# A two-layer kernel on one core: two places for the softmax's scores, half banks for the second layer's products on half chunks, and the causal mask by a select on GpSimd

## The chip, the cores and the metric

One core of one Trainium2 chip runs the whole program. The metric is device time in microseconds, from launch to the end on that core. The engines are TensorE (PE, with its weight loads as PEld), VectorE (DVE), ScalarE (ACT), GpSimd (POOL) and the queues that issue DMAs (SP's above all, and POOL's).

## The reference

The input is 2048 positions of width 128, all float32. Two layers follow each other, each with a mixer and a feed-forward part, a layernorm before each and a residual around each:

```
x = x + ssd(layernorm(x))            # layer 0: gated state-space mixer, 8 heads of 32, state 16
x = x + attention_and_experts(layernorm(x))
    # causal attention, 16 heads of 8, over all 2048 positions;
    # then 8 experts 128 -> 512 -> 128 with gelu, all computed, weighted by the two best gates
x = x + mamba(layernorm(x))          # layer 1: selective scan, inner width 128*2, state 16
x = x + ternary_ffn(layernorm(x))    # silu(x w1) * (x w2), then h1, gelu, h2, gelu, w3
```

In the attention, scores = q.k / sqrt(8), the entries with key after query are masked, softmax is taken over the keys, and the weighted sum of v follows.

## The kernel before, in words

The positions are cut into four chunks of C = 512 columns (NC = 4), each of four blocks of 128. All values stay on the chip. Every stage is written as a Python function that records operations in a `Program`: `ssd(c)`, `prepare(c)` (layernorm, q, k and v), `shift(c, g)` (the largest score of each query for head group g), `weighted(c, g)` (scores again, exp, sum over keys), `conclude(c)` (output projection), `experts(c)`, `scan(c, part)` (the selective scan on half a chunk, H = 256 columns) and `feed(c)`. The class `Order` then plays the program: it ranks every operation by the longest chain behind it, takes at each step the operation that can start first on its engine, and writes out one static order for each engine. `issue` at line 638 emits them, which is why nearly all rows of the profile carry L638. Each engine then runs its list in order, held only by semaphores.

Tiles get their memory from places. A `Tag` has a number of places, and an operation that allots a tile waits in the plan until one is free. SBUF places belong to pools: "first" (ssd), "second" (experts, scan), "attention" and "last" (feed, and a few extra tiles of scan). "second" opens when the last ssd operation is done, "last" when the last attention operation is done.

PSUM has eight banks of 512 float32 columns. The function `seat` deals them out: tag m (maxima, projections) has one place of two banks, e (scores that go to exp) one place of two banks, o (sums over keys) one bank, and a, b and c one bank each. Tag a may use banks a and b, and the banks of m while no m tile is asked for; tag c may use bank c, and those of e and o in the same way.

In `shift`, for each block of 128 queries and each chunk of keys, two thin products (32 rows deep, one for each of two heads) go into an m tile, and DVE takes the maximum over the keys. In `weighted`, for each block of 128 keys and each pair of heads, an e tile gets the thin score products, the shift by a second pair of products with `sh`, and on the diagonal a bfloat16 product with `mask_kq` that adds -1e30 where the key is after the query; ACT makes `probs` of it by exp, and four products of 128 rows by 9 columns add to o (`sum_up`). There are 320 such e tiles, 128 of them on a diagonal, 32 in each chunk.

`experts(c)` runs 8 experts in pairs on 512 columns: 4 products, 4 gelus, 4 products that accumulate, for each expert. The gelus of a pair form a batch, within which ACT takes no exp. `feed(c)` has 8 products from w1 and w2, then 16 from h1, 16 from h2, and 16 of 128 columns from w3. `scan(c, part)` runs 16 state steps: exp on ACT (`sda`), a product and two scans on DVE (`sdb`), a copy of the last state on POOL, and a DMA from POOL that adds the step's result to one of two sums (`sL`).

Of the kernel before, what the change touches and what calls it, by code (L numbers as in the profile page):

```python
# [76 lines left out]
class Place:  # L77


    def __init__(self, pool, banks=None, lent=None, real=None):  # L80
        self.pool, self.lent, self.real = pool, lent, real
        self.user, self.free = None, 0.0
        self.banks = banks or (self,)


class Tile_:


    def __init__(self, tag, shape, dtype, name, real=None):
        self.tag, self.shape, self.dtype, self.name, self.real = tag, tuple(shape), dtype, name, real  # L90
        self.log, self.first, self.place, self.left, self.last = [], None, None, 0, 0.0
        self.pe = None
        self.ops = set()
# [104 lines left out]
class Op:  # L198
    __slots__ = (
        "n", "engine", "calls", "deps", "time", "after", "table", "batch", "allots", "tiles",  # L200
        "rank", "waits", "outs", "start", "end", "ready",
# [3 lines left out]
class Program:  # L205
# [5 lines left out]
    def __init__(self, nc):  # L211
        self.nc, self.ops, self.tags, self.joined, self.batching = nc, [], {}, None, None
        for e in self.ENGINES:
            setattr(self, e, Engine(self, e))
# [14 lines left out]
    def add(self, engine, method, args, kw):  # L229
# [12 lines left out]
        for v, w in [(v, False) for v in reads] + [(v, True) for v in writes]:  # L242
# [21 lines left out]
            t.ops.add(op)  # L264
            op.tiles.add(t)
# [6 lines left out]
    def new(self, engine, table=None):  # L272
# [4 lines left out]
        op.n, op.deps, op.allots, op.tiles = len(self.ops), {}, [], set()  # L277
        self.ops.append(op)
        return op
# [104 lines left out]

class Order:
# [8 lines left out]
    def settle(self):  # L394
# [36 lines left out]
        for op in ops:  # L431
            for t in op.allots:
# [22 lines left out]
    def rank(self):  # L455
        ops = self.p.ops
        outs = {o: [] for o in ops}
        for o in ops:
# [3 lines left out]
            o.ready = 0.0  # L462
# [30 lines left out]
        for o in reversed(order):  # L493
# [5 lines left out]
            o.rank = r + o.after  # L499

    def possible(self, op):

        at, seen, taken = 0.0, {}, set()
        for t in op.allots:
# [7 lines left out]
            for pl in tag.places:  # L512
                if pl in taken or any(b.user is not None or b in taken for b in pl.banks):
                    continue
# [19 lines left out]
    def play(self):  # L534
        free = {e: 0.0 for e in Program.ENGINES}
        cand = {e: [] for e in Program.ENGINES}
# [13 lines left out]
        while len(self.order) < n:  # L550
            best = None
            for e, ops in cand.items():
# [3 lines left out]
                for o in ops:  # L556
                    at = max(free[e], o.ready)
# [10 lines left out]
                    if at < least:  # L568
                        least = at
                    pick.append((at, o))  # L570
                if not pick:
                    continue
                o = max((o for at, o in pick if at <= least + 1e-6), key=lambda o: self.key(o, open_batch))
# [8 lines left out]
            at, o = best  # L582
            e = o.engine
            cand[e].remove(o)
            for t in o.allots:
                t.tag.wanted -= 1
            if o.allots:
                self.possible(o)
                for t in o.allots:
                    t.tag.given += 1  # L590
                    for b in t.place.banks:
                        b.user = t
# [11 lines left out]
            o.start = at  # L604
            free[e] = at + time
            o.end = at + time - o.time + o.after
# [12 lines left out]
            for d, full in o.outs:  # L619
                d.waits -= 1  # L620
                d.ready = max(d.ready, o.end if full else o.start)
                if d.waits == 0:
                    enter(d)
            self.order.append(o)
        self.span = max(o.end for o in self.order)

# [14 lines left out]
SWITCH, BOOST = 1.28, 40.0  # L641
# [3 lines left out]
def two_layers(ctx: ExitStack, tc: tile.TileContext, a: dict, out: bass.AP):  # L645
# [19 lines left out]
    def banks(tag, bank, lent=None, width=1, shared=False):  # L665
        t = nc.tag(tag, width * C, True, shared)
        t.places.append(Place(None, bank.banks if isinstance(bank, Place) else tuple(bank), lent, None))
        return t.places[-1]

    pairs_ = {k: ps.tile([P, 2 * C], F32, name=f"ps_{k}") for k in ("m", "e")}  # L670
    single = {k: ps.tile([P, C], F32, name=f"ps_{k}") for k in ("o", "a", "b", "c")}
    bank = {}
    for k, t in pairs_.items():
        for j in range(2):
            bank[f"{k}{j}"] = Place(None, real=t[:, j * C : (j + 1) * C])
    for k, t in single.items():
        bank[k] = Place(None, real=t)

    def seat(tag, names, lent=None, width=1, shared=False, whole=None):
        t = nc.tag(tag, width * C, True, shared)  # L680
        pl = Place(None, tuple(bank[n] for n in names), nc.tags[lent] if lent else None)
        pl.real = whole if whole is not None else bank[names[0]].real
        t.places.append(pl)

    seat("m", ("m0", "m1"), width=2, whole=pairs_["m"])
    seat("e", ("e0", "e1"), width=2, whole=pairs_["e"])
    seat("o", ("o",))
    for n in ("a", "b"):
        seat("a", (n,), shared=True)
    for n in ("m0", "m1"):  # L690
        seat("a", (n,), "m", shared=True)
    seat("c", ("c",), shared=True)
    for n in ("e0", "e1"):
        seat("c", (n,), "e", shared=True)
    seat("c", ("o",), "o", shared=True)
# [51 lines left out]
    select(mask_kq, [[1, P]], 0, -1, ALU.is_ge, MASKED)  # L747
    before8 = const("before8", (P, NE, NE))
# [8 lines left out]
    LN = [("st", NB * 6, 2), ("mv", NB * 2, 2), ("rs", NB, 2)]  # L757
# [8 lines left out]
    def layernorm(z, dst, src, width=D):  # L766
# [3 lines left out]
        rs = tile_(f"rs_{z}", (P, nb))  # L770
        for b in range(nb):
# [3 lines left out]
        nc.gpsimd.tensor_tensor(rs, rs, minus_half[:, 0:nb], ALU.pow)  # L775
        for b in range(nb):
            nc.vector.tensor_scalar(
                dst[:, b, :], src[:, b, :], mv[:, b, 0:1], rs[:, b : b + 1], ALU.subtract, ALU.mult
            )
# [19 lines left out]
    for tag, words, n in (  # L799
        ("nx", NB * D, 1), ("nTa", C, 1), ("hi", C, 2), ("os", C, 2), ("sh", C, 2), ("qR", 2 * C, 3),  # L800
# [34 lines left out]
    def prepare(c):  # L835
        xn = xa[c] = tile_("xa", (P, NB, D))
# [6 lines left out]
        nc.vector.tensor_scalar(nT, pt, col("ln1_w"), col("ln1_b"), ALU.mult, ALU.add)  # L843
        qR = []
        for g in range(0, NG, 2):
            qR.append(tile_("qR", (P, 2, C), F32R))
            for w, n, dst in ((w_k, "k", kR[c][g // 2]), (w_q, "q", qR[-1])):
                pf = tile_("m" if n == "k" else "e", (P, 2, C))
                for j in range(2):
                    nc.tensor.matmul(pf[:, j], w[:, g + j], nT, start=True, stop=True)  # L850
                    hi = tile_("hi", (P, C), F32R)
                    nc.scalar.activation(hi, pf[:, j], AF.Identity, bias=col(f"b{n}", g + j))
                    nc.tensor.matmul(pf[:, j], minus[n], hi, start=False, stop=True, skip_group_check=True)
                    nc.vector.tensor_scalar(dst[:, j], pf[:, j], col(f"b{n}", g + j), None, ALU.add)
# [9 lines left out]
        held[c] = [q[:, j] for q in qR for j in range(2)]  # L864
# [4 lines left out]
    def shift(c, g):  # L869
        qR = held[c][g]  # L870
# [27 lines left out]
        nc.vector.tensor_copy(sh, pm)  # L898
        held[c, g] = sh

    def weighted(c, g):
        qR = held[c][g]
# [13 lines left out]
        for kb in range(nk):  # L916
# [3 lines left out]
            for i in range(0, 4, 2):  # L920
                pss = tile_("e", (P, 2, C))
                with nc.together(0.11 + 2 * (C - q0) / 2400.0 + 0.1 * diag):
# [4 lines left out]
                    for j in range(2):  # L927
                        hr = slice(32 * (i + j), 32 * (i + j) + 32)
                        nc.tensor.matmul(pss[:, j, q0:], onesR[hr], sh[hr, q0:], start=False, stop=not diag)
                    for j in range(2 * diag):  # L930
                        nc.tensor.matmul(pss[:, j, q0 : q0 + P], ident16, mask_kq, start=False, stop=True)
# [3 lines left out]
                )  # L935
                prs.append(pr)
# [5 lines left out]
        nc.vector.tensor_copy(os, po)  # L942
        pa = tile_("a", (P, NB, 4, HD + 1))
# [9 lines left out]
    def conclude(c):  # L953
        att = held.pop(("att", c))
        pt = transposed(att.rearrange("p b g i d -> p b (g i d)"), "a")
        aT = tile_("os", (P, C))
        nc.vector.tensor_copy(aT, pt)
# [6 lines left out]
    def attentions():  # L964
# [3 lines left out]
        for (c, g), nxt in zip(jobs, jobs[1:] + [None]):  # L968
            if g == 2 and c + 1 < NC:
# [42 lines left out]
    def ssd(c):  # L1012
# [516 lines left out]
```

## Time and profile before

| what | value |
|---|---|
| time, median of 3 runs | 1730.93 us (1716.0 to 1738.16) |
| the profiled execution, its own time | 1727.12 us |
| its span, first to last instruction | 1725.4 us |
| mean granted TensorE clock | 0.785 |
| PE busy | 1503.1 us (87%), 6350 matmuls |
| PEld busy | 670.9 us (39%) |
| DVE busy | 994.8 us (58%) |
| ACT busy | 642.9 us (37%), 56 table loads |
| POOL busy | 326.4 us (19%) |
| DMA | 91.75 MB, mean 53 GB/s |

A float32 product appears as two matmul instructions in the counts, and its operands' shapes as rows*columns of the weights and partitions x columns of what streams. Busy time of TensorE counts time in which a product is under way, at whatever clock. The granted clock is the share of full speed that the throttle gave.

### The profile page before, as it was taken

How to read it: one execution, taken by the hardware profiler on the slowest of the kernel's cores; microseconds unless marked ns; L12 is line 12 of the kernel's file. 1: busy time of each engine (PE TensorE's matmuls, PEld its weight loads, DVE VectorE, ACT ScalarE, POOL GpSimd, SP SyncE). 2: the span in 40 equal slices, each digit the busy share in tenths (PEclk: the TensorE clock that was granted, in tenths of full speed). 3: DMA queues.
4: the chain of work that ended last, by engine and by line, in shares of the span. 5: the costliest groups of instructions: out<-in, count | busy, mean ns of one | idle time of the engine just before them, and what ended most of it. 6: DMA issues, size and time to landing. Idle time of an engine off the chain costs nothing. (4 is left out here: it accounts for less than half of the span.)

```text
span 1725.4 us, 17368 instructions
## 1 busy us (share of the span) xinstructions
PE 1503.1 (87%) x6350; PEld 670.9 (39%) x6350; DVE 994.8 (58%) x1874; ACT 642.9 (37%) x873; POOL 326.4 (19%) x458
## 2 busy tenths in 40 slices
PE   6899998999999998899998899899877679995738
PEld 3554554455423343333333243233322234442323
DVE  4556557665545468667867656775454551256641
ACT  2221421432334426445453433454445433234311
POOL 4321310310000111212311111121031221103320
PEclk9887987996879959987865655799565569997769
DMA  2000000000112102524402311341042543134730
GB/s 86 1 1 1 1 1 1 1 1 1 42 36 61 51 1 56 123 67 87 97 7 46 60 36 35 95 110 42 13 84 56 99 110 98 49 114 106 157 88 6
DMA packets 77334, 91.75 MB, mean 53 GB/s; under 512 B 7040, under 2 KB 47776, under 8 KB 77248
## 3 DMA queue, kind: packets, MB, share of 16 engines
q1 hardware_dynamic: 59536, 58.11, 11.4%
q0 software_dynamic: 17280, 31.46, 10.7%
q10 hardware_dynamic: 432, 1.06, 0.2%
q8 instruction: 50, 0.82, 0.2%
q14 instruction: 36, 0.29, 0.1%
HBM read 57.90 MB, written 1.25 MB: 34 GB/s over the span
## 5 line engine op out<-in xcount | busy, mean ns | idle before, releaser
L638 DVE TENSOR_REDUCE top_a_None<-ps_m 128x2 f32<-128x1024 f32 (+3 forms) x320 | 339.7, 1062 | 285.0 <-PE ps_m L638 278.4
L638 ACT ACTIVATE probs_attention<-ps_e 128x1024 f32<-128x1024 f32 (+3 forms) x320 | 286.5, 895 | 526.9 <-PE ps_o L638 281.2
L638 PE MATMUL ps_e<-qR_attention,w_kR_attention 32*128 32x512 f32 (+3 forms) x640 | 187.8, 581 | 82.5 <-ACT probs_attention L638 80.9
L638 PE MATMUL ps_m<-w_kR_attention,qR_attention 32*128 32x512 f32 (+3 forms) x640 | 178.3, 546 | 17.4 <-DVE top_a_None L638 16.1
L638 PE MATMUL ps_o<-probs_attention,w_vv_attention 128*9 128x512 f32 (+3 forms) x1152 | 182.6, 712 | 0.2 <-ACT probs_attention L638 0.2
L638 POOL DMA_DIRECT2D sL_second<-sdb_second x114 | 99.2, 885 | 385.6 <-DVE sdb_second L638 328.6
L638 PEld LDWEIGHTS ps_e<-qR_attention,w_kR_attention 32*128 32x128 f32 x640 | 74.0, 227 | 237.9 <-ACT probs_attention L638 187.5
L638 DVE TENSOR_TENSOR_SCAN sdb_second<-sda_second,w_hlast_None,sdb_second 128x256 f32<-128x256 f32 x212 | 149.6, 739 | 7.7 <-ACT sda_second L638 5.4
L638 PEld LDWEIGHTS ps_m<-w_kR_attention,qR_attention 32*128 32x128 f32 x640 | 71.6, 217 | 211.8 <-issue 67.9
L638 PE MATMUL ps_e<-sh_attention,w_onesR_attention 32*128 32x512 f32 (+3 forms) x640 | 148.6, 459 | 0.0
L638 PE MATMUL ps_c<-h_second,fc_second 128*128 128x512 f32 x208 | 114.9, 654 | 0.6 <-DVE ye_second L638 0.6
L638 ACT ACTIVATE sda_second<-sL_second 128x512 f32<-128x512 f32 x120 | 72.7, 624 | 31.8 <-DVE sdb_second L638 18.6
L638 ACT ACT_TABLE_LOAD x56 | 71.8, 1283 | 30.2 <-PE ps_a L638 18.6
L638 DVE TENSOR_TENSOR sdb_second<-sL_second,sbb_second 128x512 f32<-128x512 f32 x101 | 68.0, 680 | 24.0 <-DMA sL_second<-sdb_second 11.1
L638 PEld LDWEIGHTS ps_e<-sh_attention,w_onesR_attention 32*128 32x128 f32 x640 | 80.8, 249 | 0.5
L638 POOL TENSOR_TENSOR acc_second<-acc_second,ye_second 128x512 f32<-128x512 f32 x28 | 36.5, 1305 | 231.3 <-DVE ye_second L638 229.8
L638 PE MATMUL ps_a<-enT_second,fc_second 128*128 128x512 f32 x128 | 77.0, 686 | 3.1 <-ACT h_second L638 2.2
L638 ACT ACTIVATE h_second<-ps_a,cols 128x512 f32<-128x512 f32 x64 | 44.0, 687 | 63.3 <-PE ps_a L638 63.2
L638 POOL COPY w_hlast_None<-sdb_second 128x2 f32<-128x2 f32 x99 | 55.6, 570 | 23.8 <-DVE sdb_second L638 23.5
L638 PE MATMUL ps_b<-enT_second,fc_second 128*128 128x512 f32 x98 | 58.8, 686 | 0.9 <-ACT h_second L638 0.8
L638 PE MATMUL ps_m<-fh_last,hw_last 128*128 128x512 f32 x120 | 58.3, 608 | 0.2 <-DVE sW_second L638 0.2
L638 PEld LDWEIGHTS <-ident 128*128 128x128 bf16 x512 | 30.6, 101 | 61.7 <-issue 50.0
(430 smaller groups left out, 2094.3 us busy)
## 6 DMA issues: line engine op xcount, KB each, us to landing
sL_second<-sdb_second POOLq DMA_DIRECT2D x114, 256.0 KB, 3.6
fc_second<-in_fc SPq DMA_DIRECT2D x64, 256.0 KB, 2.6
sbb_second<-scratch_b SPq DMA_DIRECT2D x112, 128.0 KB, 3.0
gb_second<-scratch_g SPq DMA_DIRECT2D x32, 256.0 KB, 3.3
hw_last<-in_h SPq DMA_DIRECT2D x8, 1024.0 KB, 5.3
w_last<-in_w SPq DMA_DIRECT2D x12, 256.0 KB, 3.9
sbb_last<-scratch_b SPq DMA_DIRECT2D x16, 128.0 KB, 3.4
sL_second<-sdb_last POOLq DMA_DIRECT2D x6, 256.0 KB, 4.2
```

What stands on the lines that cost most here:

```text
L638: getattr(engine, method)(*args, **kw)
```

## The change

It has these parts.

1. PSUM: m keeps two banks, e gets four (two places of two banks), o one, and one bank is lent to nobody. Tags b and c are gone. Tag a is a whole bank, a new tag d is half a bank (256 columns): each bank's two halves are places of their own, with the other as `mate`. The planner starts no product in a half while an accumulation is open in its mate. Both may borrow the banks of m, e and o.
2. The products of `experts` and `feed` run on half chunks, `experts(c, part)` and `feed(c, part)`, in d tiles; weights are loaded for each half, those of `feed` in pieces of 512 columns (tag fw, three places). `feed`'s tiles get places in pool "second" too.
3. The mask products of `weighted` go. After exp, on a diagonal, `select` on GpSimd sets the entries with key after query to 0 in the 128 columns that need it, for both heads in one instruction of 128 x 256.
4. DVE work moves: the normalising step of every layernorm becomes an ACT activation with scale and bias, for which GpSimd computes -mean * rstd in two small operations; copies and bias additions out of PSUM (nT, q and k, sh, os, aT, and scan's in_b, bd, dt_b, z) become ACT operations; scan's multiplication with D goes to GpSimd.
5. `prepare` computes only the first two head groups' q and k; `project(c, 2)` does the others when the chunk's first group is weighted, and qR has two places in place of three. scan has two sda and three sdb tiles in "second" (before: three and four), and more in "last".
6. `Order` models TensorE by a class `Array`: shapes, weight loads under products, the time lost between shapes, and a clock that halves when little was done in a window. When it holds thin or other small shapes it stays with that shape if it can. Its further switches (FILL, PAIR, ZMIN, BURST, FAST) are all off.

The core of the diff:

```diff
-    seat("m", ("m0", "m1"), width=2, whole=pairs_["m"])
-    seat("e", ("e0", "e1"), width=2, whole=pairs_["e"])
+    seat("m", ("m0", "m1"), whole=wide["m"])
+    for j in (0, 2):
+        seat("e", (f"e{j}", f"e{j + 1}"), whole=wide["e"][:, j * C : (j + 2) * C])
     seat("o", ("o",))
...
+    for n, lent in (("a", None), ("m0", "m"), ("m1", "m"), ("e3", "e"), ("e2", "e"), ("e1", "e"), ("e0", "e"), ("o", "o")):
+        seat("a", (n,), lent)
+        for half in range(2):
+            seat("d", (n,), lent, half)
...
     def possible(self, op):
...
+                if op.starts and any(b.mate is not None and b.mate.open for b in pl.banks):
+                    continue
...
     def layernorm(z, dst, src, width=D):
...
+        nc.gpsimd.tensor_tensor(nm, mv[:, :, 0], rs, ALU.mult)
+        nc.gpsimd.tensor_scalar(nm, nm, -1.0, None, ALU.mult)
         for b in range(nb):
-            nc.vector.tensor_scalar(
-                dst[:, b, :], src[:, b, :], mv[:, b, 0:1], rs[:, b : b + 1], ALU.subtract, ALU.mult
+            nc.scalar.activation(
+                dst[:, b, :], src[:, b, :], AF.Identity, bias=nm[:, b : b + 1], scale=rs[:, b : b + 1]
             )
...
     def weighted(c, g):
...
-                        nc.tensor.matmul(pss[:, j, q0:], onesR[hr], sh[hr, q0:], start=False, stop=not diag)
-                    for j in range(2 * diag):
-                        nc.tensor.matmul(pss[:, j, q0 : q0 + P], ident16, mask_kq, start=False, stop=True)
+                        nc.tensor.matmul(pss[:, j, q0:], onesR[hr], sh[hr, q0:], start=False, stop=True)
                 pr = tile_("probs", (P, 2, C))
                 nc.scalar.activation(
                     pr[:, :, q0:], pss[:, :, q0:], AF.Exp, scale=float(1.0 / np.sqrt(np.float32(HD)))
                 )
+                if diag:
+                    select(pr[:, :, q0 : q0 + P], [[0, 2], [1, P]], 0, -1, ALU.is_ge, 0.0)
...
         for (c, g), nxt in zip(jobs, jobs[1:] + [None]):
+            if g == 0:
+                project(c, 2)
...
-        ("second", "gb", C, 2), ("second", "ye", C, 2), ("second", "fc1", FF, 2), ("second", "fc2", FF, 2),
-        ("second", "h", C, 8), ("last", "h", C, 4),
+        ("second", "gb", H, 3), ("second", "ye", H, 2), ("second", "fc1", FF, 2), ("second", "fc2", FF, 2),
+        ("second", "h", H, 8), ("last", "h", H, 8), ("last", "fc1", FF, 2), ("last", "fc2", FF, 2), ("last", "gb", H, 2),
...
-        ("last", "fxn", NB * D, 1), ("last", "fnT", C, 1), ("last", "w12", 2 * FF, 1), ("last", "w3", NF * D, 1),
-        ("last", "fs", C, 2), ("last", "fh", C, 8), ("last", "hw", 4 * FF, 2), ("last", "res", NB * D, 1),
+        ("second", "fxn", H, 1), ("second", "fnT", H, 1), ("second", "fw", FF, 3), ("last", "fw", FF, 3),
+        ("second", "fs", H, 2), ("second", "fh", H, 8), ("last", "fh", H, 8), ("last", "fxn", H, 1),
...
                     for f in range(NF):
-                        ph = tile_("a", (P, C))
+                        ph = tile_("d", (P, H))
...
     for c in range(NC):
-        experts(c)
+        for part in range(SPLIT):
+            experts(c, part)
         for part in range(SPLIT):
             scan(c, part)
-        feed(c)
+            feed(c, part)
```

## The prediction, made before the changed kernel ran

> **What bounds the kernel now.** I read the page's busy table first, then its forty slices, then busy time by stage, the waits of TensorE, and last the time order in the poorest stage. The slices show TensorE at nine tenths almost everywhere up to the last quarter, with a granted clock that swings between five tenths and full:
>
> ```profile
> PE   6899998999999998899998899899877679995738
> PEclk9887987996879959987865655799565569997769
> ```
>
> I cut the span where work starts and ends in the trace: the layernorm of experts(0), the end of each chunk's attention (xa is updated at 355, 640, 1036 and 1395 us), and the tail. Columns: stretch, its length, then busy us (instructions) of PE, PEld, DVE, ACT, POOL, then granted clock, DMA share, GB/s.
>
> ```profile
> 90.00:500.00 410.00, 386.50 (x2051) 203.87 (x2052) 250.12 (x540) 126.66 (x178) 67.81 (x84) 0.83 0.03 8
> 500.00:603.00 103.00, 100.55 (x430) 36.80 (x430) 48.21 (x58) 44.95 (x53) 8.89 (x7) 0.95 0.19 52
> 603.00:862.00 259.00, 236.51 (x1012) 93.98 (x1012) 188.29 (x320) 122.09 (x164) 53.87 (x81) 0.80 0.32 71
> 862.00:1118.00 256.00, 230.46 (x942) 89.07 (x944) 171.26 (x282) 104.67 (x132) 34.80 (x59) 0.59 0.21 45
> 1118.00:1214.00 96.00, 93.58 (x406) 35.50 (x398) 59.74 (x89) 46.49 (x57) 22.53 (x29) 0.94 0.30 75
> 1214.00:1396.00 182.00, 134.78 (x546) 49.77 (x546) 88.95 (x161) 79.97 (x108) 36.34 (x58) 0.55 0.31 61
> 1396.00:1492.00 96.00, 86.64 (x208) 38.01 (x209) 29.44 (x73) 28.52 (x41) 18.53 (x19) 0.92 0.36 102
> 1492.00:1672.00 180.00, 121.99 (x365) 61.66 (x363) 105.71 (x195) 58.45 (x89) 44.36 (x57) 0.82 0.49 117
> ```
>
> So TensorE is the bound until 1396, at a poor clock where little dense work (128 rows deep, 512 columns) stands between the thin score products (32 rows): 0.95 and 0.94 where experts run, 0.59 and 0.55 where they do not. Work in full-clock us is busy time times clock; by it 603 to 1396 holds 236.5 x 0.80 + 230.5 x 0.59 + 93.6 x 0.94 + 134.8 x 0.55 = 487 us in 793. The tail is a chain: experts(3), two scans, feed(3).
>
> The waits of TensorE, and the cycle of one key block at 1300 us, show the one place of the score tile e:
>
> ```profile
> PE ps_e L638 <- ACT probs_attention L638: 81.4, 104, 2.8
> ...
> PE ps_c L638 <- POOL sL_second L638: 24.3, 2, 22.9
> ```
> ```profile
> 1300.21 0.79 PE L638 MATMUL ps_e<-qR_attention,w_kR_attention 32*128 32x512 f32 x2 [1.17 <-ACT probs_attention L638]
> ...
> 1301.53 1.02 ACT L638 ACTIVATE probs_attention<-ps_e 128x1024 f32<-128x1024 f32 x1 [0.86 <-PE ps_e L638]
> ...
> 1302.61 0.79 PE L638 MATMUL ps_e<-qR_attention,w_kR_attention 32*128 32x512 f32 x2 [1.18 <-ACT probs_attention L638]
> ...
> 1303.76 1.90 PE L638 MATMUL ps_o<-probs_attention,w_vv_attention 128*9 128x512 f32 x8
> ...
> 1306.82 0.79 PE L638 MATMUL ps_e<-qR_attention,w_kR_attention 32*128 32x512 f32 x2 [1.17 <-ACT probs_attention L638]
> ```
>
> Scores, exp of 1.02 us, and only then the next scores: 6.6 us a block, of which TensorE idles 2.35.
>
> **Second place for e.** The next scores are written while exp reads. The 2 x 1.17 us of this block go, and with them most of the 81.4 us. What is late next is the clock: the block becomes 4.2 us of half-clock TensorE work.
>
> **Mask.** 256 bf16 products go, 128 pairs (32 per chunk). In time order a pair takes 0.32 us at half clock (906.61 to 906.93) and 0.12 at full (the same form for the other mask, 569.56 to 569.68). I book 128 x 0.12 = 15.4 full-clock us, 8 of them before 603. In their place come 128 selects of 128 x 256 on POOL. The rows have 128 x 128 at 0.29 to 0.48 us, so 0.58 to 0.97 at twice the size, 74 to 124 us on an engine that is 19% busy; the engine hides that. The latency does not hide by itself: the sum over keys waits for exp and now for select, behind it on TensorE stand the next scores. Bounds: 0, and 64 blocks x 1.5 us (two selects less what the other one covers) = 96 us. I take 0.1 a block, 6 us, as thin products of the maximum stand between.
>
> **Half chunks.** experts and feed take 256 columns at a time. A 128x512 product takes 0.86 us at full clock and a 128x256 one 0.43 (1498.28 to 1498.71), so the work stays; the weight loads double, but lie under the products. Weight DMAs double from 31 to about 62 MB; DMA is at a third of its time. What is gained is reach: feed's tiles were in the pool that opens when attention ends, and now also stand in the pool open since 456. In the view of its tiles all feed products lie after 1396: 134.2 (fh_last) + 38.1 (fnT_last) + 3.8 (fxn_last) us of TensorE at clock 0.86, 151 full-clock us. Three quarters, 113, can move between the thin products.
>
> **Half banks.** e takes four banks, m two, o one; one bank stays unlent, in halves, where dense work had three (a, b, c). If a write to one half has to wait for the reader of the other, each half product can stand for up to about 0.45 us, the reader's time (the ACT row stz, 128x256, has 471 ns). The trace of before never shares a bank, so the cost is bounded by 0 and 0.45 x 430 products in the third stage (three chunks of 2 x 44 in experts, 2 x 18 in feed, about 2 x 11 in scan, less experts(0)'s first ones) = 194 us. I take 20: from 575 to 586 us a thin product of 0.43 us stands after nearly every pair of dense ones, and covers the wait. [...]
>
> **Copies and normalising to ACT, two POOL operations per layernorm.** Some 130 us leave DVE for ACT (16 x 6 normalisations of 0.34 to 0.43, evacuations of 0.4 to 0.75). Split gelus cost 160 x (2 x 0.47 - 0.69) = 40 us more, and table loads go from 56 towards 104 of 1.28 us: ACT rises from 643 to about 870. TensorE hides it, unless exp is kept out for long (second rival).
>
> **The sum, by stage.** 0 to 90: 90. 90 to 500: 321 - 8 = 313 full-clock us, / 0.83 / 0.943 = 400, and 5 for ssd's products, which share the one bank: 405. 500 to 603 is dense already: 103. Third stage: 487 + 113 - 8 = 592. Clock: dense work becomes (165 of experts x 2/3 + about 45 of scans + 113) / 592 = 45%, and slices with such a share (690 to 776: 44 of 86 us) had 0.86. Busy share: 0.877 before, less the waits on exp: 0.93. 592 / 0.86 / 0.93 = 741, against 793. Tail: experts' second half runs beside the scan, so 96 / 2 = 48; scan(3,0) took 130 (1492 to 1622) among the feeds' elementwise work, and its 16 steps need 16 x (0.68 + 2 x 0.74) = 35 us of DVE plus about 20 before them, so between 55 and 130: 85; scan(3,1) ended 49 after it; half a feed 30: 212, against 329. 90 + 405 + 103 + 741 + 212 + 20 + 6 = 1577; outside the span the profiled run has 1727.12 - 1725.4 = 1.7: **1579 us**. That run is 0.2% below the median of the three times.
>
> [...]
>
> **Rivals.**
> *Better: the clock holds.* With two places the block at full clock is 2.1 us, nearly half of it 128 rows deep. Third stage at 0.95 and 0.95: 656; tail 190; second stage 385: 90 + 385 + 103 + 656 + 190 + 2 = 1426. For it: 0.97 and more in the slices where experts run beside scores. Against: with one m place, DVE's reduce of 1.22 us still paces the maxima.
>
> *No gain: dense work is used up early.* The order still takes dense work as soon as it is ready, and 1288 to 1396 stays thin. Clock of the third stage as before, 487 / 695 = 0.70: 592 / 0.70 / 0.93 = 909, in all 1747. For it: scan(2) and experts(2) were gone by 1290. Against: each feed becomes ready only after its scan. ACT kept busy by gelu batches (twice as many, each with two table loads) would end near here too.
>
> *Slower: the halves are one place.* Each of 584 half products of the second layer (430 and the tail's 154) stands 0.45 us: 1579 - 20 + 263 = 1822. It decides from 0.35 us a product (1764). For it: one unlent bank for all dense work. Against: thin work to cover it until 1396, and lent banks afterwards.
>
> That the change does not move feed at all (no room before 1396) is part of the no-gain case.
>
> **How the numbers follow.** Forecast 0.50, with 1500 to 1690 of its own; better 0.25; no gain 0.12; halves 0.13. Faster by over 2% is below 1696, slower above 1766; 2% is about what a measurement of this kernel tells from no change. Faster: 0.49 + 0.25 + 0.03 = 0.77; same: 0.01 + 0.09 = 0.10; slower 0.13. The range leaves a tenth on either side: from 1430, just above the better case, to 1740, by the no-gain case and inside the bank bound of 1579 + 174 = 1753.
>
> **What would show it.** Right: fh_last products from about 750 us on; waits of ps_e for probs below 20 us; clock between 862 and 1396 above 0.8; the last conclude some 50 us earlier and a tail near 210. Wrong: TensorE waiting on h or fh readers for over 100 us, a clock still under 0.65 before attention ends, or sums waiting for POOL.

## The result and the profile after

The changed kernel takes 1820.5 us (median of four runs, 1800.2 to 1841.1), the kernel before 1724.2 on the same chips. The ratio is 1.051, 95% interval 1.038 to 1.065: 5% slower, where 1579 us was forecast. The profiled execution took 1800.2 us with a span of 1798.5. In some executions the granted clock is lower and the time longer (1841.1 us at 0.794, against 1800.2 at 0.825); the ratios leave these out, the medians do not.

The page of the changed kernel (busy time, and two rows of the forty slices):

```profile
PE 1455.9 (81%) x6926; PEld 792.7 (44%) x6926; DVE 912.1 (51%) x1726; ACT 817.3 (45%) x1345; POOL 439.6 (24%) x731
...
PE   6898998999888998887788887878876677675676
...
PEclk9797698789779888776899776799876889977688
```

TensorE is busy for 47 us less than before and has a better clock from the middle on, and yet the span is 73 us longer: its idle time rose from 222 us (1725.4 - 1503.1) to 343. The last quarter, which had three slices at nine tenths before, has none above seven. The waits of TensorE (us in total, times, longest):

```profile
PE ps_a L811 <- ACT h_second L811: 73.8, 103, 1.5
PE ps_e L811 <- ACT probs_attention L811: 45.5, 53, 2.1
PE ps_a L811 <- DMA fw_second<-in_h: 38.0, 9, 10.6
PE ps_m L811 <- DVE top_a_None L811: 27.6, 36, 3.5
...
PE ps_a L811 <- DVE fh_second L811: 15.2, 15, 2.9
```

The wait for exp fell from 81.4 to 45.5. New is the first line: products (of experts) held until a gelu has read the tile that stood there. Before, it read

```profile
PE ps_a L638 <- ACT h_second L638: 2.2, 5, 0.8
```

In the names, h and fh are the hidden tiles of experts and feed, fc and fw the pieces of their weights.

Attention now ends at 1351 us, before at 1396. Cut there, busy time by stretch, first before, then after (stretch, length, busy us of PE, PEld, DVE, ACT, POOL, granted clock, DMA share, GB/s):

```profile
0.00:1396.00 1396.00, 1251.07 (x5662) 551.40 (x5662) 850.94 (x1591) 546.69 (x730) 261.02 (x379) 0.77 0.19 43
1396.00:1725.40 329.40, 252.07 (x688) 119.45 (x688) 143.90 (x284) 96.16 (x143) 65.42 (x79) 0.86 0.38 95
```
```profile
0.00:1351.00 1351.00, 1147.03 (x5808) 577.29 (x5808) 755.46 (x1411) 671.72 (x1061) 346.59 (x589) 0.83 0.22 52
1351.00:1798.50 447.50, 308.85 (x1118) 215.46 (x1118) 156.60 (x316) 145.54 (x285) 92.97 (x144) 0.82 0.47 113
```

Read each line as work (busy time of TensorE x clock, in us at full clock) and idle time. Up to the end of attention the work is about the same (963 and 952 full-clock us); the clock gained, idle time went from 145 to 204. The tail is 118 us longer: 36 more work, 61 more idle, and the rest a lower clock. A scheduler that plans a whole kernel reacts to any edit everywhere, so below I compare stages by these two numbers, not only totals.

### The profile page after: what moved, and what is told of

The parts are those of the page before. It is cut to its first block, busy times and chain, and to the rows that moved or that the text cites. A ratio compares the mean times of both kernels' runs of the same rounds, so it can differ in the third digit from the quotient of the medians.

```text
span 1798.5 us, 19537 instructions
## 1 busy us (share of the span) xinstructions
PE 1455.9 (81%) x6926; PEld 792.7 (44%) x6926; DVE 912.1 (51%) x1726; ACT 817.3 (45%) x1345; POOL 439.6 (24%) x731
## 5 line engine op out<-in xcount | busy, mean ns | idle before, releaser
L811 PE MATMUL ps_a<-enT_second,fc_second 128*128 128x256 f32 x436 | 146.9, 452 | 60.2 <-ACT h_second L811 52.5
L811 ACT ACTIVATE h_second<-ps_a,cols 128x256 f32<-128x256 f32 x236 | 102.2, 471 | 160.3 <-PE ps_a L811 148.0
L811 PE MATMUL ps_e<-qR_attention,w_kR_attention 32*128 32x512 f32 (+3 forms) x640 | 126.4, 516 | 42.5 <-ACT probs_attention L811 40.0
L811 PE MATMUL ps_a<-h_second,fc_second 128*128 128x256 f32 x368 | 120.0, 449 | 19.3 <-DVE ye_second L811 8.1
L811 PEld LDWEIGHTS ps_a<-enT_second,fc_second 128*128 128x128 f32 x436 | 79.9, 209 | 112.1 <-ACT h_second L811 90.6
L811 POOL TENSOR_TENSOR acc_second<-acc_second,ye_second 128x256 f32<-128x256 f32 x56 | 46.0, 821 | 300.4 <-DVE ye_second L811 289.0
L811 POOL TENSOR_SCALAR_AFFINE_SELECT probs_attention<-probs_attention 128x256 f32<-128x256 f32 x128 | 57.8, 464 | 232.3 <-ACT probs_attention L811 224.4
L811 PE MATMUL ps_e<-sh_attention,w_onesR_attention 32*128 32x512 f32 (+3 forms) x640 | 103.6, 417 | 0.0
L811 PE MATMUL ps_a<-fh_second,fw_second 128*128 128x256 f32 x176 | 62.5, 472 | 46.4 <-DMA fw_second<-in_h 38.0
L811 PEld LDWEIGHTS ps_a<-h_second,fc_second 128*128 128x128 f32 x368 | 73.5, 217 | 51.9 <-ACT h_second L811 14.8
```

Of the source, the lines that this page charges most:

```text
L811: getattr(engine, method)(*args, **kw)
```

## The experiments

Ratios are against the kernel before, run on the same chip, with 95% intervals. "Tail" is the time from the end of attention to the end of the span. Part 5 of the change, and the new numbers of SBUF places by themselves, no run takes alone.

**1 and 2: are the halves of a bank places of their own?** The first run gives a d tile a whole bank:

```diff
-        for half in range(2):
-            seat("d", (n,), lent, half)
+        seat("d", (n,), lent)
```


> The changed kernel with one edit: a d tile takes a whole bank, so two half products never stand in one bank. Theory A (the two halves of a bank are one place: a product into one half waits for the reader of the other): the halves gave no room, so nothing is lost by giving them up; 1770 to 1840 us beside the changed kernel's 1820, and TensorE's waits on readers of h and fh stay within a third of 74 + 15 us, now as waits for the whole bank. Rival (the halves are places that work, and the loss comes from something else): half the room for dense products is gone, so these waits double or more and the time goes above 1880.

1800.8 us, 1.048 (1.042 to 1.054). The loss of all half places cost nothing in total, as theory A has it; but waits of ps_a on h fell to 25 us, further than the third that it allowed. The tail fell to 370 us, and attention ended at 1433, so two changes of about 80 us cancel.

The second names the lower half of every bank before any upper half:

```diff
     for n, lent in lendable:              # the same list of eight banks, now with a name
         seat("a", (n,), lent)
-        for half in range(2):
+    for half in range(2):
+        for n, lent in lendable:
             seat("d", (n,), lent, half)
```


> The changed kernel with one edit: the list of places names the lower half of every bank before any upper half, so the plan fills different banks first where banks are free. Theory A (halves are one place): after the attention, where m, e and o are free, successive half products stand in different banks; the idle 0.93 us per pair goes there, the tail of 449 us falls by 50 to 100, and the total is 1720 to 1780. In the attention, with one bank unlent, little changes. Rival (the tail is long because of its work, weight transfers and the scan's chain, not because of the banks): tail and total stay within 20 us of the changed kernel.

1740.3 us, 1.014 (1.010 to 1.018): 80 us for the order of a list. The tail fell from 447 to 365, as theory A said. In both runs the plan of the first layer had moved as well (its last layernorm from 473 to 550 and 569 us), which runs 13 and 14 take out.

**3, 5, 6: why feed stayed in the tail.** In the changed kernel the first products on fh (feed's h1) start after attention; the view of the tile (count, duration min/median/max, first and last start):

```profile
L811 PE MATMUL ps_m<-fh_second,fw_second x192: 379/379/796, 1358.7 to 1791.1; 128*128 128x256 f32 x192
L811 PE MATMUL ps_a<-fh_second,fw_second x176: 379/379/795, 1357.7 to 1790.3; 128*128 128x256 f32 x176
```

The third run gives feed a higher rank (`RAISE = {"feed": 2000.0}`), the fifth a fourth place of fw as well (`("second", "fw", FF, 4), ("last", "fw", FF, 2)`), the sixth also the order of halves of run 2.

> The changed kernel with one edit: feed's operations get a higher rank, so the plan takes them as soon as they can start, from about 1000 us on for the first chunk. Theory B (the loss is that the plan leaves all four feeds behind the attention): fh products from about 1010 us on, the tail falls by 60 to 110 us, attention ends 10 to 40 later, total 1730 to 1790. Theory A alone (the halves stall wherever they stand): the stalls move with the products; total 1790 to 1840.

1826.9 us, 1.061 (1.055 to 1.068). The fh products still start only at 1386.8: rank was not what held them.

> The changed kernel with feed's raised rank, as in the run with the raised rank alone, and one digit more: the pool open since the ssd has four places of fw in place of three (the later pool two in place of three). Theory B2 (feed was not held back by its rank but by this digit: the four gelus after h1 form a batch whose four weight pieces are allotted together, so with three places the first fh products wait for the pool that opens when attention ends): fh products from about 810 to 830 us on, about half of all of them before attention ends, the tail falls from some 440 to 340 or below. As the moved half products still stand in half banks that wait for each other, attention ends 60 to 100 us later, total 1740 to 1810. Rival (something else holds feed back, such as room in the banks): first fh products still after 1350, total within 20 us of 1827.

1808.6 us, 1.053 (1.045 to 1.060), and this in the view of the tile:

```profile
L811 PE MATMUL ps_a<-fh_second,fw_second x312: 379/379/796, 802.7 to 1801.5; 128*128 128x256 f32 x156
```

With one place of fw more in the pool open before, the products start at 803. The planner's function `settle` gives all tiles of a batch that are not in PSUM to its first operation; h1's batch of four gelus needs four fw pieces at once, and the pool open before attention ends had three. But the time hardly moved: attention ends 103 us later (1454), the tail is 356, with 320 of the 640 product instructions on fh in each.

> As the run before it, and the list of places names the lower half of every bank first, as in the run that named them so. Theory A with B2: the two repairs add up, since one acts on the tail's stalls and the other on what lies in the tail: 1660 to 1720 us, under the kernel before (1716). Rival (the move of feed only shifts time from the tail into the attention, as the one unlent bank is full there): 1730 to 1760, as with the order of places alone.

1776.2 us, 1.032 (1.024 to 1.040): a miss for both, slower than the 1740 without the move. Busy time by stretch, run 2 and then run 6:

```profile
0.00:1377.00 1377.00, 1168.33 (x5808) 590.12 (x5808) 773.77 (x1432) 683.33 (x1070) 369.29 (x604) 0.81 0.22 53
1377.00:1741.90 364.90, 281.10 (x1118) 199.25 (x1118) 140.55 (x295) 138.54 (x275) 84.22 (x128) 0.90 0.52 131
```
```profile
0.00:1479.80 1479.80, 1251.38 (x6232) 652.71 (x6232) 778.69 (x1444) 713.62 (x1130) 359.32 (x599) 0.84 0.23 56
1479.80:1773.70 293.90, 185.81 (x694) 127.89 (x694) 143.19 (x283) 114.68 (x219) 98.07 (x133) 0.81 0.53 125
```

About 102 full-clock us left the tail (253 to 151), and 105 came into the attention (946 to 1051). The attention paid full price, 103 us: none of its 209 us of idle time was filled. The tail gave back only 71: its idle time rose from 84 to 108 us and its clock fell from 0.90 to 0.81. What stays there is experts(3) and two scans; that they are a chain which feed's products had been filling is the likely reading.

Run 11 leaves the raised rank out and is otherwise run 6. It was expected at 1700 to 1735 us if the rank had put feed ahead of the work that sets the end, and at 1735 to 1780 if moved work costs the attention what the tail gains at any rank. It took 1754.9 us, 1.015 (1.007 to 1.022), which is no gain over run 2 (1.014). In its profiled execution, the fastest of four, about a fifth of the products on fh had moved; attention ended 31 us later than in run 2 and the tail was 41 us shorter. So the second case holds, and part of run 6's loss is the rank, or the larger share that it moved.

**4, 7, 9, 10, 12: the parts one by one.** The mask by select in the kernel before, all else as it was:

> The kernel before with one edit: the 256 mask products of the attention go, and a select on GpSimd after exp takes their place; one place for e, all else as before. Theory A or B (the select is not the loss): 128 pairs of 0.12 to 0.32 us go from TensorE, the select's latency stands partly in the way of the sums; 1695 to 1730 us beside 1724. Rival C (the select's wait for GpSimd costs what the prediction's upper bound said): 1740 to 1820, with waits of ps_o for POOL of more than 20 us.

1714.0 us, 0.998 (0.994 to 1.002). No clear gain and no loss; sums wait 0.6 us in all for POOL.

The new planner in the kernel before:

> The kernel before with the changed kernel's class Order and its model of TensorE, and nothing else of the change. Theory A (the loss is in the banks): the order gains or loses little, 1690 to 1740 us beside 1716. Rival D (the new model writes a worse order, whatever the banks): 1760 to 1840.

1752.2 us, 1.020 (1.013 to 1.027): between the two. Half chunks in the kernel before, in whole banks (`experts(c, part)`, `feed(c, part)`, d tiles taken from tags a and c), with the changed kernel's SBUF places and two copies, enT and fnT, on ScalarE:

> The kernel before with one part of the change: experts and feed on half chunks, in whole banks of the tags a and c as before, with the changed kernel's SBUF places; one place of e, the old order, the mask products and the copies on DVE stay. Theory A (the loss is in banks shared by halves): half chunks cost only their extra gelu overhead and table loads on ScalarE, 1700 to 1750 us beside 1716. Rival G (half chunks themselves cost: twice the weight transfers and twice the gelu batches, each of which keeps exp out): 1760 to 1850.

1778.5 us, 1.031 (1.026 to 1.036): inside rival G's range. Their stretches up to the end of attention, planner and then half chunks:

```profile
0.00:1413.50 1413.50, 1270.98 (x5670) 572.39 (x5670) 862.72 (x1603) 550.09 (x731) 278.81 (x387) 0.75 0.19 44
```
```profile
0.00:1438.00 1438.00, 1264.67 (x6072) 630.25 (x6072) 871.77 (x1671) 604.37 (x864) 272.53 (x415) 0.77 0.22 52
```

The planner's loss there is clock (0.75 against 0.77; idle 143 against 145), and its tail is 341 us against 329. Half chunks add 28 us of idle time and some 11 of work (the clock's two digits leave about 6 either way); table loads go from 56 to 85, of 1.28 us each. What carries the 28 us no run separates.

The copies and normalising steps back on DVE in the changed kernel (`nc.scalar.activation(...)` and `nc.scalar.copy(...)` of part 4 undone):

> The changed kernel with one part undone: the layernorms' normalising step, the copies and bias additions out of PSUM, and scan's multiplication with D are on DVE again. Theory A (ScalarE's load is no part of the loss): within 20 us of the changed kernel's 1820. Rival H (ScalarE at 817 us is on the path: exp and the gelus that free the half banks come late behind the copies): 1740 to 1790, and TensorE's waits on h and probs fall by a third.

1857.2 us, 1.073 (1.064 to 1.081), and with the halves of run 2:

> The changed kernel with the lower halves named first, and the DVE work back on DVE. If ScalarE's load adds to the wait for half banks, 1690 to 1725 us; if it has no part in the loss, within 15 us of the 1740 with the places alone.

1766.2 us, 1.020 (1.010 to 1.029) against 1.014. All four cases were missed. Undone, the kernel is slower: by some 2% in the first pair (the intervals just touch), by less than the intervals tell in the second. So the work that moved to ScalarE shows no part in the loss.

**8: the second place of e.** One place for e and whole banks for d, so that e2 and e3 are banks nobody lends:

```diff
-    for j in (0, 2):
+    for j in (0,):
         seat("e", ...)
-    for n, lent in (("a", None), ("m0", "m"), ("m1", "m"), ("e3", "e"), ("e2", "e"), ...):
+    for n, lent in (("a", None), ("e3", None), ("e2", None), ("m0", "m"), ("m1", "m"), ...):
         seat("a", (n,), lent)
-        for half in range(2):
-            seat("d", (n,), lent, half)
+        seat("d", (n,), lent)
```


> The changed kernel with one place for e, as before; its two banks become whole places that nobody lends, so dense work has three unlent banks; d tiles take whole banks. Theory A: TensorE waits for exp 80 us or more as in the kernel before, and the dense work no longer waits for its banks (waits on h and fh readers under 20 us); the two nearly cancel against the run with whole banks and two places of e (1801): 1760 to 1830. Rival E (the second place of e is worth the 80 us of waits and more, as the clock holds with it): 1850 to 1900. Rival F (the second place of e was worth nothing and cost banks): 1680 to 1740.

1994.6 us, 1.163 (1.154 to 1.173): above every case. Up to the end of attention, run 1 (two places of e) and this one:

```profile
0.00:1433.00 1433.00, 1227.67 (x5808) 601.12 (x5808) 779.75 (x1432) 689.62 (x1072) 357.11 (x604) 0.78 0.21 50
```
```profile
0.00:1638.60 1638.60, 1384.25 (x5816) 657.11 (x5816) 788.23 (x1456) 704.60 (x1074) 364.48 (x619) 0.71 0.19 46
```

So the second place of e, against two unlent banks, is worth 206 us here: 49 of idle and 157 of busy time. About 120 of the 157 are clock (0.78 against 0.71), the rest more work (983 against 957). TensorE waited 131 us for exp here and 55 there, so the direct wait is the smaller part. With three free banks dense work can also be taken early and be missing later; this run does not part that from the e tile itself.

**13 and 14: the halves in the second layer alone.** A tag s of their own for the products of experts, scan and feed, on the same banks, so that the first layer's plan stays:

```diff
+    for half in range(2):
+        for n, lent in (("a", None), ("m0", "m"), ...):
+            seat("s", (n,), lent, half)
...
-                        ph = tile_("d", (P, H))
+                        ph = tile_("s", (P, H))
```


> The changed kernel, with the lower halves named first for the second layer's products alone (a tag of their own on the same banks); the first layer's keep the changed kernel's places, and so its plan until about 470 us. Theory A (the halves of a bank are one place, and the tail is where other banks are free): the tail stays near the 365 us of the run with all halves spread, the early stages near the changed kernel's, and attention ends near 1350: 1690 to 1730 us. Rival (the gain of that run came with its other plan of the first layer): 1770 to 1820.

1684.3 us, 0.981 (0.972 to 0.991): faster than either kernel, though an edge of 2% is not proven. The stretches, cut at the end of attention:

```profile
0.00:1326.50 1326.50, 1141.86 (x5808) 578.30 (x5808) 767.61 (x1428) 676.30 (x1067) 359.34 (x602) 0.83 0.22 54
1326.50:1687.10 360.60, 278.18 (x1118) 197.61 (x1118) 143.46 (x299) 138.83 (x276) 87.31 (x130) 0.91 0.53 134
```

The tail holds the same 253 full-clock us as in the changed kernel and takes 87 us less: 56 of idle, 31 of clock. The same work in time order, products of an expert's first matrix in the tail, in the changed kernel and in this one (start, duration, idle before it in brackets; x4 is two products, x2 one):

```profile
1429.07 1.13 PE L811 MATMUL ps_a<-enT_second,fc_second 128*128 128x256 f32 x4 [0.56 <-ACT h_second L811]
1431.13 1.13 PE L811 MATMUL ps_a<-enT_second,fc_second 128*128 128x256 f32 x4 [0.93 <-ACT h_second L811]
1433.19 1.13 PE L811 MATMUL ps_a<-enT_second,fc_second 128*128 128x256 f32 x4 [0.93 <-ACT h_second L811]
```
```profile
1353.00 0.59 PE L811 MATMUL ps_m<-enT_second,fc_second 128*128 128x256 f32 x2
1353.73 0.70 PE L811 MATMUL ps_a<-enT_second,fc_second 128*128 128x256 f32 x2
1354.26 0.60 PE L811 MATMUL ps_m<-enT_second,fc_second 128*128 128x256 f32 x2
1354.99 0.70 PE L811 MATMUL ps_a<-enT_second,fc_second 128*128 128x256 f32 x2
```

With two products in one bank, TensorE writes both halves, stands 0.93 us until both gelus (0.47 us each) have read them, and writes again: 2.06 us a pair. The first gelu waits too: it starts at 1430.24, when the second product has ended, though its own half was written about half a microsecond before (an estimate: the first of the two products starts at 1429.07, and a single one, as at 1427.81, takes 0.70 us). With two banks in turn the pair takes 1.26 us, and no wait stands in these rows. The planner knows nothing of this: it takes a half as free once its own tile is read, and holds back only products that would start beside an open accumulation. In the tail of the changed kernel the waits on h were

```profile
PE ps_a L811 <- ACT h_second L811: 21.4, 24, 1.1
PE ps_a L811 <- ACT fs_second L811: 13.3, 13, 1.2
PE ps_a L811 <- DVE fh_second L811: 12.8, 13, 2.9
```

and in the tail of this run

```profile
PE ps_a L811 <- DVE fh_second L811: 2.0, 2, 1.2
PE ps_a L811 <- ACT h_second L811: 2.0, 4, 0.7
```

The rows above put the price of two halves of one bank, written and read in pairs, at 0.93 us of idle TensorE a pair here. The waits in them are for semaphores, that is for the order that the program carries; what the chip does where nothing orders two halves, no run here shows.

Before the end of attention, where only one bank is always free, run 13 takes away much less: waits on h come to 37 us there, 52 in the changed kernel.

The same with whole banks in the place of halves:

```diff
-            seat("s", (n,), lent, half)
+        seat("s", (n,), lent)
```


> The changed kernel, with whole banks for the second layer's products alone and halves for the first layer's. Theory A (in the second layer a half bank is worth no more than a whole one shared): attention ends within 20 us of the changed kernel's 1350 and the tail is near 365: 1700 to 1740 us. Rival (half places do give room beside the scores, and whole places lose it): attention ends at 1420 or later, total 1780 to 1810, as with whole banks everywhere.

1752.3 us, 1.023 (1.018 to 1.028): between the cases.

```profile
0.00:1381.00 1381.00, 1199.89 (x5808) 591.19 (x5808) 774.22 (x1421) 681.35 (x1065) 352.28 (x596) 0.79 0.21 51
1381.00:1752.50 371.50, 280.82 (x1118) 199.94 (x1118) 148.59 (x306) 144.66 (x283) 90.20 (x136) 0.88 0.54 134
```

The tail is nearly as good (372), but attention ends 54 us later, with the same work (948) and the same idle time (181 and 185): the difference is clock, 0.79 against 0.83. So theory A was right for the tail and wrong for the attention. That half places let dense products stand more often between the scores, where only one bank is to be had, and that this holds the clock, is a guess: the order of products differs, and no run shows what in it makes the difference.

**15 and 16: the planner's rule to stay with a shape.**

```diff
                     if keep and (...):
-                        now = keep
+                        pass
```


> The kernel before with the changed kernel's class Order but without its rule to stay with the shape that TensorE holds; the kernel with the rule had a ratio of 1.020. Theory K (the rule costs the 2%, as it takes thin products in a row and leaves dense ones for later): 1700 to 1730 us, a ratio within 1% of one. Rival (the model's times cost it): 1745 to 1770.

1763.6 us, 1.031 (1.024 to 1.038) against 1.020 (1.013 to 1.027) with the rule: no gain without it.

> As the run with the lower halves named first for the second layer alone, without the rule to stay with the shape that TensorE holds. Theory K: 20 to 40 us less than that run, so 1660 to 1700, under the kernel before. If the rule pays once e has two places, as thin products then stand in rows anyway: the same or up to 30 us more.

1764.5 us, 1.032 (1.022 to 1.042) against 0.981. Theory K falls twice, and in run 16's kernel the rule clearly pays. What in the new model costs the kernel before its 2% stays open; how near its times and its clock come to the chip's is not shown here.

**17 and 18: what is left in the best version.** `("last", "fw", FF, 4)` in place of 3, and then `("second", "fw", FF, 4)` too:

> As the run with the lower halves named first for the second layer alone (1684 us), with four places of fw in the pool that opens after the attention in place of three, seven in all in the tail. TensorE's waits for pieces of feed's weights came to 33 us there. If they are what holds the tail now, they fall below 20 us and the time is 1660 to 1680; if a transfer waits for something else than a place, such as the queue it stands in, nothing changes: 1675 to 1695.

1694.7 us, 0.989 (0.982 to 0.997): no gain; TensorE's waits for feed's weight pieces stayed at 36 us (35 in run 13), so a fourth place is not what they lack.

> As the run beside it, and four places of fw in the pool open since the ssd too, so that the first chunk's feed can pass its batch before attention ends. Theory B (moving feed is worth what the prediction booked, once the banks no longer collide): attention ends 15 to 40 us later, the tail is 40 to 70 shorter, 1640 to 1670 us. Rival (as in the run with raised rank, the attention gives back what the tail gains): 1675 to 1700.

1682.7 us, 0.973 (0.962 to 0.984), against 0.981 (0.972 to 0.991) for run 13: the intervals overlap, and 0.973 rests on two executions (1659 and 1680 us). Products on fh start at 1261, so little moves, and its worth cannot be told from nothing. Runs 13 and 18 are the fastest versions; the intervals of both lie below the kernel before.

## Why the prediction was wrong, step by step

Three terms of the sum failed: the third stage's busy share, the wait of half banks, and the tail with feed's move in it. Up to the end of attention 90 + 405 + 103 + 741 + 20 + 6 = 1365 us were forecast, and 1351 came; the tail was forecast at 212 and took 447.5. The profiled execution's whole error of 221 us looks like the tail's 235, but the first number is right by luck: two errors cancel in it.

**Feed's move failed.** The step "now also stand in the pool open since 456 ... three quarters, 113, can move" counted places and not the batch, which takes four pieces where three places stand. All feed products stayed in the tail. At the forecast's own rates, 113 / 0.86 / 0.93 = 141 us should then be missing before 1365, that is 1224; 1351 came, 127 more. Nor was the move a gain in the sum itself: it put 141 us on the third stage and took at most 329 - 212 = 117 off the tail. What the sum drew from it was dense work for the clock. Runs 5, 6 and 11 agree that the move gains nothing: in run 6 the attention gave 103 us and the tail gave back 71. With over half of feed's products gone from it, the tail still took 294 us and not 212.

**Half banks were mis-sized,** 20 us within 0 to 194 for the third stage and nothing for the tail. In the third stage the waits on h alone came to 43.9 us; in the tail those on h, fs and fh above, with 5.3 on h_last, come to 53. The mechanism was named and its unit was right (0.45 us a product forecast, 0.93 a pair measured). The reason for the low value, that thin products cover the wait and "lent banks afterwards" help in the tail, held in part before the tail and not in it: the list of places names both halves of a bank before the next bank, so in the tail, with seven more banks free, products still go in pairs into one. The profiled executions of the changed kernel and of run 13 differ by 1798.5 - 1687.1 = 111 us, 87 in the tail and 24 before it (the medians by 136). The slower rival's 1822 met the time by luck: its mechanism is right, but it took all 584 products as stalled and feed as moved. Of the no-gain rival one condition held, that feed does not move; its clock of 0.70 did not, and its 1747 counts feed as moved.

**Half chunks were booked at nothing** ("so the work stays"): 3.1% in run 9. **The planner was described and not priced:** 2.0% in run 7. Both are measured on the kernel before; what they cost beside two places of e no run shows.

**TensorE's busy share** in the third stage, forecast 0.93, was 615 of 748 us, 0.82:

```profile
603.00:1351.00 748.00, 615.19 (x3170) 291.62 (x3162) 461.10 (x767) 432.59 (x665) 193.26 (x329) 0.82 0.34 76
```

Without feed the forecast's rates give 479 / 0.86 / 0.93 = 599 us here, so 149 us came on top: 91 of idle time, 58 of busy time. Of the 133 idle us, 44 are the waits on h, 36 on exp and 18 on DVE's maxima. The forecast took away the waits on exp and put 20 us of half banks in their place. The clock was 0.82 against the 0.86 forecast and 0.69 before, and it came without feed's dense work, which the forecast had counted on for it; run 8 (0.71 up to the end of attention, 0.78 in run 1) points to the second place of e as its source, as far as it parts that from the banks. The waits for exp fell only to 45.5 us in the whole, not below 20: late in the attention a thin block still stands for exp, as in time order at 1301 us:

```profile
1300.90 0.50 PE L811 MATMUL ps_e<-qR_attention,w_kR_attention 32*128 32x512 f32 x2 [2.11 <-ACT probs_attention L811]
1301.23 0.40 PE L811 MATMUL ps_e<-sh_attention,w_onesR_attention 32*128 32x512 f32 x2
1301.56 1.07 PE L811 MATMUL ps_o<-probs_attention,w_vv_attention 128*9 128x512 f32 x8
```

**The select** takes 464 ns, less than both its bounds (0.58 to 0.97 us), and its latency shows none of the 6 us booked (the sums wait 0.8 us in all for POOL); nor do the removed mask products show as a gain (0.998 in run 4). **ScalarE** came out near the forecast (817 us against 870, 84 table loads against 104), and by runs 10 and 12 TensorE does not pay for it. The groups of the changed kernel:

```profile
L811 ACT ACT_TABLE_LOAD x84 | 107.8, 1283 | 37.8 <-PE ps_m L811 11.9 <-PE ps_a L811 8.6 <-DVE acc_second L811 7.2
...
L811 POOL TENSOR_SCALAR_AFFINE_SELECT probs_attention<-probs_attention 128x256 f32<-128x256 f32 x128 | 57.8, 464 | 232.3 <-ACT probs_attention L811 224.4 <-PE ps_a L811 6.8
```

Of the signs named ahead, the fh products from 750 us on, the waits of ps_e and the tail of 210 went wrong; the clock above 0.8 and the earlier end of attention came true. The threshold of 100 us for waits on h and fh was missed narrowly: 73.8 + 5.3 + 15.2 = 94.

## What to carry to other kernels

A place in a plan is only as good as the order that the program keeps on it: before splitting a PSUM bank, ask who reads the other half (0.93 us of idle TensorE a pair here), and let the allocator take a fresh bank before a second half (87 us of tail between the changed kernel and run 13). Where an allocation is made for a group at once, count the group against the pool, not the tile. And before work is moved, price it at both ends: in run 6 the attention paid 103 us for what gave the tail 71.

## What the runs showed of the hardware that was not expected

Idle gaps seem to cost twice. The tail's 253 full-clock us ran at 0.82 with 139 us of gaps among them and at 0.91 with 82 (run 13); in runs 8, 2, 1 and 14, with 247 to 254 us of work, the clock fell from 0.93 over 0.90 and 0.88 to 0.88 as the gaps grew from 80 over 84 and 85 to 91. Gaps are not all: up to the end of attention runs 13 and 14 had equal work (948 full-clock us) and about equal idle time (185 and 181 us) and differed by 54 us through the clock (0.83 and 0.79). A select over 128 x 256 float32 took 464 ns, no more than the slowest of the single ones over 128 x 128 float32 (0.30, 0.33 and 0.48 us).
